# The scan states of a chunk fetched at the end of a loop turn instead of in its middle, with the scan steps spread anew over the turns

## The chip, the cores and the metric

The kernel runs on one core of a Trainium2 chip. The metric is the device time of one execution in microseconds. Five engines work side by side, each in the order of its own instruction stream: PE (matrix multiply; PEld is its weight load), DVE (vector), ACT (scalar and activation functions), POOL, and SP, which in this kernel only issues DMA transfers. They meet through semaphores. An instruction that waits holds up everything behind it on its engine.

## What is computed

The input `x` is 2 x 4096 x 256, read as 8192 tokens of 256 values. Cut to what matters:

```python
u = x @ W_in + b_in                       # 64 values a token
g = sigmoid(x @ W_gate + b_gate)
h_t = tanh(h_prev @ A + u_t @ Bm)         # scan over tokens in time
y = g * (h @ C.T + u @ D.T) + (1 - g) * x
x1 = layernorm(x + (y @ W_out + b_out + x))
hh = gelu(x1 @ (alpha1 * sign(w1)).T + b1)   # 1024 wide
out = layernorm(x1 + hh @ (alpha2 * sign(w2)).T + b2)
```

`alpha1` and `alpha2` are the mean absolute values of the rows of `w1` and `w2`. All in float32. The scan runs along each of the two sequences of 4096 tokens, from a zero state.

## The kernel before

**The scan.** Each sequence of 4096 tokens is cut into 64 segments of 64 tokens, so that the two sequences give 128 columns which are scanned side by side. One *step* (L163 to L165) is one matmul of the 128 x 128 matrix made of A and Bm with the 128 columns (PE, two passes), then a tanh on ACT that writes the next state into `st`. There are 40 warm-up steps, that bring the segments' first states near their true values, and 64 real ones: 104 in all, in the order of the list `plan`; `done` counts them. The lower half of `st` holds `u`, the upper half the states.

**The chunks.** Everything else is done in 16 chunks of 512 tokens; one chunk takes four steps' states. For a chunk c the stages are:

- `load_u` (L353) and `load_h` (L357): DMAs that copy u and the states of the chunk out of `st` into the two halves of the tile `hu` (three buffers). `load_x` (L345), `load_gate_x` (L104): x transposed. `load_n` (L362): x as rows into `xn` (four buffers; so the fetch for chunk c+3 waits until the store of chunk c-1, which leaves from the same buffer, has landed).
- `gate`: matmuls `ps_g` and a tanh `tg` (L372). `mix`: two output tiles `ps_y` from `hu` and `cd` (L381, four matmul passes), the add of a row to `xn` on POOL (L366), then d on DVE (L388); `mix_end` (L393, L396).
- `project`: 16 matmul passes `ps_z` (L406), then x1 (L417) and its statistics (L262, L266, L271, and on POOL L272). `shift` (L277) and `norm` (L285, four ACT passes).
- `blocks`: a transpose in blocks of 32 on DVE (L456) and 16 DMAs of 32 KB on the SP queue (L462) which put x1 transposed into `xlo`; `split_hi` (L470, ACT) and `split_lo` (L474, DVE) cut it in two parts.
- `up` in four pieces (8 matmul passes L493 each; gelu L503 and a cast L512 on ACT), `low` (L519, DVE), `down` in four pieces (16 matmuls L535 each), the scaling L551, `add` (L557), `stats`, and `store`: `shift`, four ACT passes (L285), the output DMA (L572, SP).

**The order.** It is written out by hand in the loop `for c in range(end)` (c = 0 to 14), and no scheduler changes it: each engine's instructions stand in the order in which the program emits them, SP's DMAs included. A turn c works at the same time on the up and down products of chunk c, the last half of down and the store of chunk c-1, norm and blocks of chunk c+1, mix and project of chunk c+2, and the fetches of chunk c+3. For turn c, left to right in the order of the text:

norm and blocks c+1; up 0; down 2 of c-1; **mix c+2**; mix_end; **load c+3** (u, then states); load_x; up 1; step; down 3 of c-1; add, stats of c-1; gate; up 2; step; split_hi c+1; store c-1; **load_n c+3**; down 0; project c+2; up 3; step; down 1.

`step()` (L680) emits one step if there is one left. `do(i, "load")` first emits steps until all states of chunk i are in the plan's past, then the two DMAs. In turns 10 and 11 one more step stands just ahead of `mix`. So the loop begins with 66 steps done; turns 0 to 9 hold three steps, turns 10 and 11 four, and from turn 12 on there are none.

Of the kernel before, what the change touches and what calls it, by code (L numbers as in the profile page):

```python
# [37 lines left out]
def gated_recurrence_then_binary_ffn(  # L38
# [61 lines left out]
    def load_xT(c, pieces=1):  # L100
        x_tiles[c] = xp.tile([P, KD, N], FP, tag="xt", name=f"xt{c}", bufs=XTB)
        for k in range(pieces):
            cut = slice(k * KD // pieces, (k + 1) * KD // pieces)
            nc.sync.dma_start(out=x_tiles[c][:, cut, :], in_=xT[c][:, cut, :])  # L104
# [53 lines left out]
    def idle_products(n):  # L158

        for _ in range(n):  # L160
            nc.tensor.matmul(p_h, ones, ones, start=True, stop=True)
# [20 lines left out]
    def count():  # L182
        nc.tensor.matmul(p_h[0:1, 0:1], ones[:, 0:1], cnt[:, 0:1], start=True, stop=True)
        nc.vector.tensor_copy(flag, p_h[0:1, 0:1])
# [59 lines left out]
    def mean_w2():  # L244
        ps = p_1.tile([P, N], FP, tag="h", name="ps_al2")
        nc.tensor.matmul(ps[:, :DM], ones, al2[:, 0, :], start=True, stop=True)
        nc.vector.tensor_scalar(al2_r, ps[:, :DM], 1.0 / H, None, ALU.mult)
        yield
# [396 lines left out]
    ch = [Chunk(c, f"{c}") for c in range(NC)]  # L645
# [8 lines left out]
    def ready():  # L654
        return done < len(plan) and plan[done] // SPC in have_u

    def next_steps():
        nonlocal done
        steps(plan[done])
        done += 1  # L660
        if done == WARM:
            first_states()
        for i in range(3):
            if done == WARM + (i + 1) * SPC:
                ch[i].load_h()
        if waiting and not held:
            for what, args in waiting:
                what(*args)
            waiting.clear()

    def emit(what, pieces, pace=5600):
        nonlocal since
        for _ in pieces:
            since += COST.get(what, 0)
            if since >= pace:
                since = min(since - pace, pace // 2)
                if ready():
                    next_steps()

    def step():  # L680
        if ready():
            next_steps()

    def do(i, what, *args, pace=5600):
        if not 0 <= i < len(ch):
            return
        if what == "load":
            need = WARM + (ch[i].c + 1) * SPC
            while done < need:
                next_steps()  # L690
            ch[i].load_u()
            ch[i].load_h()
        elif what in ("load_n", "load_x", "load_gate_x"):
            getattr(ch[i], what)()
        else:
            emit(what, getattr(ch[i], what)(*args), pace)
# [4 lines left out]
    def parts(n, pace):  # L701
        emit("part", (next(stream) for _ in range(n)), pace)
# [31 lines left out]
    with tc.manual_schedule(engines={ET.PE, ET.Activation, ET.DVE, ET.Pool, ET.SP}):  # L734
        waiting = []
        for c in range(FIRST + 1, FIRST + 6):
            load_xT(c)
        idle_products(7)
        emit("u", u_of_chunks((FIRST,)), 1 << 30)
        since = 0  # L740
        for p in range(48):
            for visit in VISITS.get(p, ()):
                emit("", u_of_chunks(*visit))
                emit("u", [None], EARLY)
            for what, *args in AROUND.get(p, ()):
                what(*args)
            parts(1, EARLY)
        assert done >= WARM + SPC, done
        for i in range(6):
            ch[i].xt = x_tiles[i]  # L750
        ch[0].in_x = ch[1].in_x = True
        parts(1, 600)
        do(0, "mix", pace=850)
        do(0, "mix_end")
        held = True
        parts(2, 600)
        assert done >= WARM + 2 * SPC, done
        do(1, "mix", pace=850)
        do(1, "mix_end")
        held = False  # L760
        do(0, "project", 0, p_2, "o", pace=1700)
        do(0, "project", 1, pace=1700)
        do(0, "stats1")
        assert done >= WARM + 3 * SPC, done
        do(2, "mix", pace=1700)
        do(0, "shift")
        do(1, "project", 0, p_2, "o", pace=1700)
        do(0, "norm")
        do(1, "project", 1, pace=1700)
        do(1, "stats1")  # L770
        parts(2, 1700)
        while waiting:
            next_steps()
        waiting = None
        do(0, "turn", True)
        emit("", mean_w2())
        mixed = ch[2].mix_end()
        next(mixed)
        do(1, "norm", nc.vector)
        do(0, "rest")  # L780
        next(mixed)
        parts(3, 1700)
        end = len(ch) - 1
        parts_met = compare()
        since = -1 << 40
        size[0] = TB
        for c in range(end):
            far = 0 < c < end - 1
            if far:
                do(c + 1, "shift")  # L790
                do(c + 1, "norm")
                do(c - 1, "low", 3)
                do(c + 1, "blocks")
            do(c, "up", 0)
            if c == end - 1:
                do(c - 1, "low", 3)
                do(c + 1, "shift")
                do(c + 1, "norm")
            do(c - 1, "down", 2)
            if c > 0:  # L800
                if c in (10, 11):
                    step()
                do(c + 2, "mix")
            do(c, "low", 0)
            mixed = ch[c + 2].mix_end() if 0 < c < end - 1 else iter(())
            next(mixed, None)
            if c == end - 1:
                assert done == len(plan), done
                next(parts_met)
                next(parts_met)  # L810
            do(c + 3, "load")
            do(c + 6, "load_x")
            if c > 0 and c % 2 == 0:
                do(10 + c // 2, "load_gate_x")
            do(c, "up", 1)
            step()
            do(c - 1, "down", 3)
            next(mixed, None)

            if c <= 12 or c == end - 1:  # L820
                do(c - 1, "add")
            if c <= 12:
                do(c - 1, "stats")
            if 2 <= c <= 12:
                emit("gate", (next(stream) for _ in range(KD)))
            if c == 0:
                do(c + 1, "turn")
            do(c, "low", 1)
            if c == end - 2:
                do(c - 1, "add")  # L830
            if c > 12:
                do(c - 1, "stats")
            if c == end - 1:
                next(parts_met)
                next(parts_met)
            if c < end - 2:
                do(c + 1, "rest")
            do(c, "up", 2)
            if c == end - 1:
                do(c + 1, "turn")  # L840
                do(c + 1, "rest")
            step()
            if far:
                do(c + 1, "split_hi")
            do(c, "low", 2)
            if c < end - 2:
                do(c - 1, "store", range(TB), nc.scalar)
            do(c + 3, "load_n")
            do(c, "down", 0)
            do(c + 2, "project", 0)  # L850
            if c == end - 2:
                do(c + 1, "split_lo")
                ch[c - 1].st2.shift(range(TB))
            do(c + 2, "project", 1)
            if far and c < end - 2:
                do(c + 1, "split_lo")
            do(c + 2, "stats1")
            if c == end - 2:
                do(c + 1, "rest")
            do(c, "up", 3)  # L860
            if c >= end - 2:
                do(c - 1, "store", range(TB), nc.scalar)
            step()
            do(c, "down", 1)
        count()
        do(end, "up", 0)
        do(end - 1, "low", 3)
        do(end, "low", 0)
        do(end - 1, "down", 2)
        do(end - 1, "down", 3)  # L870
        do(end, "up", 1)
        do(end - 1, "add")
        do(end - 1, "stats")
        do(end, "low", 1)
        do(end, "up", 2)
        do(end, "low", 2)
        do(end, "down", 0, True)
        do(end, "up", 3, True)
        do(end - 1, "store", range(TB), nc.scalar)
        do(end, "low", 3, True)  # L880
        do(end, "down", 1)
        do(end, "down_end")
# [64 lines left out]
```

## Time and profile before

| | us |
|---|---|
| median of 3 runs | 434.62 (433.52 to 434.92) |
| the profiled execution, its own time | 433.8 |
| its span (first to last instruction) | 431.9 |
| from one `mix` to the next, turns 2 to 13 (127.08 to 371.77) | 22.24 in the mean |

| engine | busy us | share of the span |
|---|---|---|
| PE | 421.8 | 98% |
| PEld | 343.0 | 79% |
| DVE | 334.9 | 78% |
| ACT | 283.1 | 66% |
| POOL | 162.6 | 38% |

How to read it: the span is that of one profiled execution; 1.9 us lie around it. The chain of work that ended last is followed back from the last instruction, at each step to what released it. In an answer in order of time a row has the start, the duration, the engine, the line, the operation and what it writes from what; SPq stands for the issue of a DMA on the SP queue, not for its transfer. In the page's DMA rows the last number is the median time from issue to landing. In the answer on waits a row has the waiting engine and line, what released it, the time in total, the number of waits and the longest.

### The profile page before, as it was taken

The page shows a single profiled execution, that of the slowest core. Times are in us where ns is not written, and L with a number is a line of the kernel's source. Part 1 is how long each engine was busy: PE and PEld are TensorE (multiplying, and loading weights), DVE is VectorE, ACT ScalarE, POOL GpSimd, SP SyncE. Part 2 cuts the span into 40 slices and gives each one's busy share as a digit, 9 for nine tenths or more (in the row PEclk, how much of TensorE's full clock was granted, in tenths as well). Part 3 has the DMA queues.
Part 4 walks back from the last instruction along what each step waited for, and adds up shares of the span by engine and source line. Part 5 has one row for each costly group of instructions (what it writes and reads, how often), then busy time and mean ns, then how long its engine had stood idle before and what let it go on. Part 6 is the DMA issues. An engine that isn't in the chain of part 4 may idle for free.

```text
span 431.9 us, 6782 instructions
## 1 busy us (share of the span) xinstructions
PE 421.8 (98%) x2390; PEld 343.0 (79%) x2390; DVE 334.9 (78%) x569; ACT 283.1 (66%) x472; POOL 162.6 (38%) x176
## 2 busy tenths in 40 slices
PE   8999999999999999999999999999999999999992
PEld 6576667788978888887878787979797888889981
DVE  0255377885979797979898888888797979799684
ACT  3353533486576777767676867677777685859881
POOL 1000013564143545353535454534343444415513
PEclk9999999999999999999999999999999999999996
DMA  8894555000251625161525242524242232311102
GB/s 288 312 286 181 159 154 176 1 2 0 45 176 41 219 52 179 42 227 36 155 65 187 78 143 77 191 74 146 71 128 87 58 115 58 114 34 50 49 2 102
DMA packets 30902, 49.24 MB, mean 114 GB/s; under 512 B 5264, under 2 KB 19600, under 8 KB 30864
## 3 DMA queue, kind: packets, MB, share of 16 engines
q1 hardware_dynamic: 30288, 48.39, 35.7%
q8 instruction: 21, 0.34, 0.3%
q10 hardware_dynamic: 576, 0.37, 0.3%
q14 instruction: 17, 0.14, 0.1%
HBM read 29.33 MB, written 8.39 MB: 87 GB/s over the span
## 4 chain that ended last, share of the span: by engine, by line
PE 96%; DMA 1%; DVE 1%; ACT 0%; SPq 0%; POOLq 0%; POOL 0%; issue 0%; DVEq 0%
PE ps_h L493 27%; PE ps_o L535 26%; PE ps_g L320 13%; PE ps_z L406 13%; PE ps_y L381 6%; PE ps_s L164 6%; PE ps_u L138 3%; DMA w_gate<-in_W_gate 1%; PE ps_t L437 1%; PE ps_p L535 0%; DVE hlo L519 0%; DVE bs_b L262 0%; SPq L104 0%; ACT h L503 0%; POOLq L886 0%; POOL rs_b L272 0%
## 5 line engine op out<-in xcount | busy, mean ns | idle before, releaser
L535 PE MATMUL ps_o<-sg,hhi 128*128 128x256 f32 x496 | 120.5, 284 | 0.0
L535 PE MATMUL ps_o<-sg,hlo 128*128 128x256 f32 x496 | 117.4, 278 | 0.1
L503 ACT ACTIVATE h<-ps_h,bias_c,al 128x512 f32<-128x512 f32 x128 | 95.0, 770 | 14.9 <-PE ps_h L493 10.7
L366 POOL TENSOR_TENSOR xn<-xn,bo_r 128x256 f32<-128x256 f32 x64 | 59.0, 955 | 100.6 <-DMA xn<-in_x 97.6
L535 PEld LDWEIGHTS ps_o<-sg,hhi 128*128 128x128 f32 x496 | 93.4, 188 | 1.4 <-DVE o L551 0.4
L535 PEld LDWEIGHTS ps_o<-sg,hlo 128*128 128x128 f32 x496 | 93.4, 188 | 1.4 <-DVE hlo L519 0.3
L493 PE MATMUL ps_h<-xhi,sg 128*128 128x512 f32 x256 | 92.7, 443 | 0.0
L519 DVE TENSOR_TENSOR hlo<-h,hhi 128x1024 fp32r<-128x1024 f32 (+1 forms) x65 | 79.9, 1247 | 4.9 <-ACT hhi L512 4.6
L493 PE MATMUL ps_h<-xlo,sg 128*128 128x512 f32 x256 | 79.8, 393 | 0.0
L512 ACT CAST hhi<-h 128x1024 fp32r<-128x1024 f32 (+1 forms) x65 | 67.4, 1039 | 2.0
L272 POOL TENSOR_TENSOR rs_b<-rs_b,neg_half 128x4 f32<-128x4 f32 (+1 forms) x17 | 28.1, 1655 | 102.0 <-DVE rs_b L271 97.0
L320 PE MATMUL ps_g<-xt,w_gate 128*128 128x384 f32 (+3 forms) x212 | 66.1, 425 | 0.3 <-DMA w_gate<-in_W_gate 0.3
L493 PEld LDWEIGHTS ps_h<-xhi,sg 128*128 128x128 f32 x256 | 46.5, 189 | 18.6 <-issue 9.8
L165 ACT ACTIVATE st<-ps_s 64x128 f32<-64x128 f32 x104 | 27.8, 267 | 45.0 <-PE ps_s L164 44.6
L493 PEld LDWEIGHTS ps_h<-xlo,sg 128*128 128x128 f32 x256 | 48.0, 188 | 11.1 <-DVE xlo L474 0.2
L366 POOL TENSOR_TENSOR xn<-xn,b_r 128x256 f32<-128x256 f32 x64 | 55.4, 895 | 1.9 <-PE ps_t L437 1.9
L406 PE MATMUL ps_z<-w_out,tg 128*128 128x256 f32 x224 | 50.7, 379 | 0.0
L164 PEld LDWEIGHTS ps_s<-st,wab 128*128 128x128 f32 x208 | 35.4, 189 | 19.1 <-ACT st L165 10.1
L406 PEld LDWEIGHTS ps_z<-w_out,tg 128*128 128x128 f32 x224 | 41.4, 190 | 5.1
L470 ACT CAST xhi<-xlo 128x1024 fp32r<-128x1024 f32 x13 | 13.7, 1051 | 42.4 <-DMA xlo<-xb 26.6
L164 PE MATMUL ps_s<-st,wab 128*128 128x128 f32 x208 | 40.6, 277 | 0.1
L320 PEld LDWEIGHTS ps_g<-xt,w_gate 128*128 128x128 f32 x212 | 33.2, 191 | 7.2 <-issue 5.3
(79 smaller groups left out, 485.2 us busy)
## 6 DMA issues: line engine op xcount, KB each, us to landing
xt<-in_xT SPq DMA_DIRECT2D x31, 512.0 KB, 4.3
xn<-in_x SPq DMA_DIRECT2D x16, 512.0 KB, 3.2
out_y<-xn SPq DMA_DIRECT2D x15, 512.0 KB, 2.6
xlo<-xb SPq DMA_DIRECT2D x208, 32.0 KB, 1.9
hu<-st SPq DMA_DIRECT2D x32, 128.0 KB, 2.3
w1t<-in_w1T SPq DMA_DIRECT2D x2, 512.0 KB, 5.8
w1n<-in_w SPq DMA_DIRECT2D x2, 512.0 KB, 6.7
w2t<-in_w2T SPq DMA_DIRECT2D x2, 512.0 KB, 6.5
```

The lines of the kernel that those rows point to most:

```text
L164: nc.tensor.matmul(p_h, ab, st[:, j].rearrange("p b k -> p (b k)"), start=True, stop=True)
L165: nc.scalar.activation(h_of[:, j + 1].rearrange("p b k -> p (b k)"), p_h[TOP, :], AF.Tanh)
L272: nc.gpsimd.tensor_tensor(rs, rs, neg_half[:, cut], ALU.pow)
L320: nc.tensor.matmul(ps[:, cut], w_gate[:, k, bass.ts(m, P)], xt_[:, k, cut], start=k == 0 and i == 0, stop=k == KD - 1, skip_group_check=True,)
L366: nc.gpsimd.tensor_tensor(r[:, i, :], r[:, i, :], row, ALU.add)
L381: nc.tensor.matmul(ps[:, m, :], cd[:, bass.ts(m, P)], self.hu, start=True, stop=True)
L406: nc.tensor.matmul(self.ps_z[:, i, :], self.y[:, k, bass.ts(i, P)], w_out[:, k, :], start=k == 0, stop=k == KD - 1,)
L493: nc.tensor.matmul(ps, sg1[:, k, bass.ts(j, P)], part[:, k, :], start=n == 0, stop=n == 2 * KD - 1,)
L503: nc.scalar.activation(to, ps.rearrange("p (a i c) -> p a i c", a=P // 32, c=32) if self.far else ps, AF.Gelu, bias=b1_c[:, j : j + 1], sc ...
L512: nc.scalar.copy(hi[:, part, :], h[:, part, :])
L519: nc.vector.tensor_sub(lo[:, i, :], h[:, i, :], hi[:, i, :].bitcast(FP))
L535: nc.tensor.matmul(ps[:, i, :], part[:, j % 2, bass.ts(tb, P)], sg2[:, j, :], start=j == 0 and part is self.h[j // 2][0] and first, stop=j ...
```

## The change

`load` is taken apart. `load_u` stays where `load` stood, in the middle of the turn. `load_h`, with the steps it makes sure of, goes to the end of the turn, between the third step and `down 1`. On the SP queue this puts L357 behind the store of chunk c-1 and behind `load_n` of chunk c+3. The extra step in turns 10 and 11 goes, and so does the second step of turn 1; the three steps stand in turn 12 instead. So a turn holds three steps, turn 1 two, until turn 12; the step's instructions are the same. L353 to L572 keep their numbers in the changed kernel.

```diff
-        if what == "load":
+        if what == "load_h":
             need = WARM + (ch[i].c + 1) * SPC
             while done < need:
                 next_steps()
-            ch[i].load_u()
             ch[i].load_h()
-        elif what in ("load_n", "load_x", "load_gate_x"):
+        elif what in ("load_u", "load_n", "load_x", "load_gate_x"):
             getattr(ch[i], what)()
...
             if c > 0:
-                if c in (10, 11):
-                    step()
                 do(c + 2, "mix")
...
-            do(c + 3, "load")
+            do(c + 3, "load_u")
             do(c + 6, "load_x")
...
-            step()
+            if c != 1:
+                step()
             if far:
                 do(c + 1, "split_hi")
...
             step()
+            do(c + 3, "load_h")
             do(c, "down", 1)
```

## The prediction

> **What bounds the kernel now.** I read the chain of work that ended last first, then the busy time by stretch of the main loop, then the SP queue and the matrix engine in order of time.
>
> ```profile
> span 431.9 us, 6782 instructions
> PE 421.8 (98%) x2390; PEld 343.0 (79%) x2390; DVE 334.9 (78%) x569; ACT 283.1 (66%) x472; POOL 162.6 (38%) x176
> PE 96%; DMA 1%; DVE 1%; ACT 0%; SPq 0%; POOLq 0%; POOL 0%; issue 0%; DVEq 0%
> xn<-in_x SPq DMA_DIRECT2D x16, 512.0 KB, 3.2
> out_y<-xn SPq DMA_DIRECT2D x15, 512.0 KB, 2.6
> xlo<-xb SPq DMA_DIRECT2D x208, 32.0 KB, 1.9
> hu<-st SPq DMA_DIRECT2D x32, 128.0 KB, 2.3
> ```
>
> 96% of the chain is PE, so PE's own order sets the time. The table of stretches says the same of the loop: in the turns from 125 to 414 us PE is busy in all of every stretch (22.40 of 22.40, 22.30 of 22.30, 21.70 of 21.70), at a granted clock of 1.00. Nothing is hidden there: PE has no idle time to give back, and each microsecond that it is made to wait in the loop goes straight to the end. From the DMA rows keep the landing times, counted from issue: 3.2 us for `xn`, 2.3 for a half of `hu`.
>
> The last turn that matters, c = 12, on the SP queue and then on PE:
>
> ```profile
> 362.58 0.60 SPq L353 DMA_DIRECT2D hu<-st  x1
> 363.28 0.54 SPq L357 DMA_DIRECT2D hu<-st  x1
> 367.12 0.35 SPq L572 DMA_DIRECT2D out_y<-xn  x1
> 369.78 0.33 SPq L362 DMA_DIRECT2D xn<-in_x  x1
> 373.58 10.48 SPq L462 DMA_DIRECT2D xlo<-xb  x16
> ```
> ```profile
> 371.77 1.88 PE L381 MATMUL ps_y<-hu,cd 128*128 128x512 f32 x4
> ```
> ```profile
> SPq L572 <- ACT xn L285: 36.3, 13, 6.8
> SPq L362 <- DMA out_y<-xn: 29.3, 12, 3.4
> ```
>
> The reader is to see: the states (L357) are issued 8.5 us ahead of the matmul that reads them (L381, `mix` of chunk 15, in turn 13). The `xn` fetch (L362) is issued only 2.0 us ahead of it, because it reuses the buffer that the store (L572) writes out, and waits 2.66 us for that store to land. The store in turn waits for ACT.
>
> **Part 1, the steps.** PE's order has 38 steps in the loop before and after, 104 in all. One leaves turn 1, one each leaves turns 10 and 11, and three enter turn 12. On PE a step shows as a hole of 0.22 us between its neighbours (turn 11: the step starts at 327.57, `mix` at 327.79), wherever it stands. Sum: -3 x 0.22 + 3 x 0.22 = 0. In none of the 38 places does PE wait for the step before (that wait, 10.1 us in 30 cases on the page of waits, is 0.2 us in one case after 84 us), since steps stand 3.8 us or more apart. ACT's 0.27 us tanh moves likewise. In turn 12 ACT is busy 15.67 of 21.70 us, so three more are covered; uncovered they would cost 0.8 us.
>
> **Part 2, `load_u`.** It stays in place. With L357 gone from behind it, the next fetches (L345, L104) go 0.64 us sooner, and are needed turns later: nothing. The store is not drawn forward: SP stands idle ahead of L572 in every turn, waiting for ACT.
>
> **Part 3, `load_h`, the whole price.** SP issues in order. In the changed order the states of chunk c+3 come directly behind `load_n` of c+3 (L362), which itself stands behind the store's landing. So their issue cannot come before that of L362, n, plus 0.35 to 0.40 us. The last tanh that turn 12's fetch needs falls at about 369.8 by ACT's queue (the cast that ends 369.51, then 0.27), not later than n: no further delay. Behind `load_h` on SP stand the 16 `xlo` fetches, which wait for DVE's transpose until 3.4 us or more after n: not delayed. Behind the waiting `mix` stands all of PE.
>
> When do the states land? Lower end: 0.40 + 2.3 = n + 2.7, as if alone. Upper end: behind the 512 KB of `xn`, n + 3.3 + 0.6 = n + 3.9. The nearest row is two 512 KB fetches issued back to back at 142.54 and 143.17 (L345, L104): they land 4.0 and 4.5 us after issue, that is at 146.54 and 147.67, 1.13 us apart, against 3.5 us for a single one issued at 163.99. The second is served after the first. So I take 3.2 for `xn` and about 0.5 us for 128 KB more (32 KB land in 1.9, 128 KB in 2.3: 0.4 us for 96 KB): **n + 3.7**.
>
> The page "DMA: Bandwidth & Descriptors" of the Trainium skill, section "Queues, rings and completion order", speaks against the change too: descriptors on each DMA engine are consumed in ring order. By it the sum would use n + 3.7, without it n + 2.7; the pair of rows above decides without the page.
>
> Lateness against the trace, turn by turn (start of `mix` minus n gives the gap; late = 3.7 - gap):
>
> turn of `mix`: n, start, gap, late
> 2: 126.18, 127.08, 0.90, 2.80
> 3: 149.03, 149.33, 0.30, 3.40
> 4: 169.79, 171.57, 1.78, 1.92
> 5: 191.63, 193.82, 2.19, 1.51
> 6: 214.18, 216.07, 1.89, 1.81
> 7: 236.96, 238.31, 1.35, 2.35
> 8: 258.96, 260.56, 1.60, 2.10
> 9: 280.46, 282.81, 2.35, 1.35
> 10: 302.69, 305.27, 2.58, 1.12
> 11: 325.04, 327.79, 2.75, 0.95
> 12: 348.14, 350.08, 1.94, 1.76
> 13: 369.78, 371.77, 1.99, 1.71
>
> If each were paid in full: 22.8 us. But a stall in turn c moves turn c+1's `mix` too, while n of turn c hangs mainly on `project` of the turn before, by `norm`, the transpose (L456) and 11 us of `xlo` issue to `split_hi` (L470) and the store's ACT pass (L285). So the last stall is deducted from the next lateness. Not without limit: that ACT pass also needs `nm_b` (L277), which hangs on this turn's PE work. Its end stands 0.4 to 1.5 us ahead of the pass, 0.9 in the mean, and DVE's backlog ahead of it adds about 0.3; I let the deduction reach 1.2 us. Then the stalls are 2.80, 2.20, 0.72, 0.79, 1.02, 1.33, 0.90, 0.45, 0.67, 0.28, 1.48, 0.51: **13.2 us**. The profiled execution took 433.8 us (span 431.9 and 1.9 around it); 433.8 + 13.2 = **447.0**. It lies 0.8 under the median of 434.62, which I leave as spread.
>
> Does PE's clock fall in stalls this long? In the tail, 420 to 424 us holds 0.77 us without a matmul at clock 1.00, and 424 to 432 us none at all at 0.59. I cost it at nothing; the longest stall expected, 2.8 us, lies between these. The Trainium skill's page "TensorE: Matmul & The Clock Gate", section "What's actually happening", puts the fall at an idle window of about 3.4 us; by that only a stall longer than any of mine would cost more.
>
> **Rivals.**
> - *Main, 0.62.* Landing at n + 3.7 with deduction: 447.0. With an unlimited deduction (only the two-turn path counts) the same lateness gives 11.5 us, 445.3. For it: the pair of fetches; against: no 128 KB copy behind a 512 KB fetch is in the trace.
> - *The states are not held up behind `xn`, 0.17.* Landing at n + 2.7: stalls 1.80, 1.20, 0.51, 0.30, 1.05, 0.05, 0.30, 0.76, together 6.0 us: 439.8. For it: the 2.3 us row; against: the pair.
> - *Nothing is deducted, 0.16.* If the store's pass waits for this turn's PE work each time, every lateness is paid: 433.8 + 22.8 = 456.6. For it: ACT waits for `nm_b` ahead of L470 in two turns; against: it waits for `xlo` in seven.
> - *Not slower, 0.05: the fetch lands in time.* Place: the same wait of `mix`. With a landing of n + 1.5 or less almost only turns 2 and 3 would wait, about 1.2 us together. At the best even the three steps taken off turns 1, 10 and 11 count and those of turn 12 are free: -0.7 us, 433.1. Against it: the shortest landing on the page is 1.9 us for 32 KB, and even that plus 0.4 is late in turns 2 and 3 by 1.4 and 2.0.
> - That the change doesn't do what it says is excluded by the order: steps stand three to a turn, two in turn 1, to turn 12, and L357 stands behind L362 in every turn from 0.
>
> **How the numbers follow.** Predicted is the main case. The range takes in both bounds of the landing and of the deduction: 439.8 to 456.6, rounded to 439.5 and 457; only "not slower" is outside. 0.3% of 434 us is 1.3 us, about what a measurement of this kernel can tell from no change. Only the fourth case lies within or under that: slower 0.95, same 0.03, faster 0.02.
>
> **What would show it.** Right: PE idle ahead of L381, released by the DMA `hu<-st`, in most of twelve turns and largest in turns 2 and 3; L357 0.4 us behind L362 on SP; that DMA's landing up from 2.3 to about 3.3 us; PE's busy time unchanged; the chain showing some 3% of DMA `hu<-st`. Wrong: a landing still at 2.3 us (second case), or stalls near the full lateness each turn (third), or a granted clock under 1.00 inside the loop, which I cost at nothing.

## The result, and the profile after

The changed kernel takes 452.93 us (median of 6 runs, 450.85 to 453.51), the one before 434.50 us (6 runs): 1.0417 times as long, with a 95% interval from 1.0398 to 1.0436. The profiled execution took 453.51 us, 19.7 more than that of before, and its span is 451.7 us, 19.8 more.

The page of the changed kernel: the span, the busy times, the chain that ended last by engine, and three DMA rows (the last number is the time from issue to landing).

```profile
span 451.7 us, 6779 instructions
PE 426.8 (94%) x2390; PEld 345.1 (76%) x2390; DVE 325.8 (72%) x569; ACT 284.7 (63%) x472; POOL 146.1 (32%) x176
PE 47%; DMA 14%; DVE 13%; SPq 12%; ACT 8%; issue 4%; POOL 1%; POOLq 0%; DVEq 0%; ACTq 0%
...
xn<-in_x SPq DMA_DIRECT2D x16, 512.0 KB, 3.6
out_y<-xn SPq DMA_DIRECT2D x15, 512.0 KB, 2.6
...
hu<-st SPq DMA_DIRECT2D x32, 128.0 KB, 2.6
```

PE does the same 2390 instructions but is no longer the chain: 47% of it instead of 96%, and the rest is shared among the DMAs, the SP queue, DVE and ACT. PE's idle time is the span less its busy time: 24.9 us instead of 10.1. So 14.8 of the 19.8 us are idle, and 5.0 are longer busy time, of which more below. The median of the `hu` row has risen little, since half of those 32 transfers are `load_u`, which did not move.

The waits of PE on this tile (us in total, times, longest):

```profile
PE ps_y L381 <- DMA hu<-st: 11.7, 11, 2.0
...
PE ps_y L381 <- issue: 3.1, 1, 3.1
```

That is the whole 14.8 us, in twelve waits, one for each `mix` of turns 2 to 13. The 3.1 us of turn 2 are the same wait, for which the profile names no releaser: its states are issued at 127.03 and land 3.7 us later, and `mix` starts at 130.83.

Turn 12 on the SP queue, and `mix` of turn 13 on PE, as they were shown of before:

```profile
385.12 0.34 SPq L572 DMA_DIRECT2D out_y<-xn  x1
387.80 0.34 SPq L362 DMA_DIRECT2D xn<-in_x  x1
388.23 0.55 SPq L357 DMA_DIRECT2D hu<-st  x1
```
```profile
392.03 1.99 PE L381 MATMUL ps_y<-hu,cd 128*128 128x512 f32 x4 [0.74 <-DMA hu<-st]
```

The states (L357) are now issued 3.8 us ahead of `mix` instead of 8.5, directly behind the rows (L362). The chain of waits in the stretch from 196 to 204 us has the mechanism from end to end (start, duration, what):

```profile
195.80 0.99 ACT xn L285 x2
...
196.81 2.62 DMA out_y<-xn
...
199.49 0.33 SPq L362
...
199.87 3.79 DMA hu<-st
...
203.71 0.70 PE ps_y L381
```

Read downwards: ACT's last pass of the store, the store's landing, the issue of the rows fetch into the buffer that the store has left, then 3.79 us for the states, then PE.

Measured from the rows issue, n, to the start of `mix`, the twelve turns give 4.18, 4.36, 3.90, 4.22, 4.15, 4.14, 3.89, 4.34, 4.31, 4.21, 4.21 and 4.23 us: 4.2 in the median, where the prediction had 3.7.

### The profile page after: what moved, and what is told of

It is laid out like the page before. It is cut to its first block, busy times and chain, and to the rows that moved or that the text cites. A ratio compares the mean times of both kernels' runs of the same rounds, so it can differ in the third digit from the quotient of the medians.

```text
span 451.7 us, 6779 instructions
## 1 busy us (share of the span) xinstructions
PE 426.8 (94%) x2390; PEld 345.1 (76%) x2390; DVE 325.8 (72%) x569; ACT 284.7 (63%) x472; POOL 146.1 (32%) x176
## 4 chain that ended last, share of the span: by engine, by line
PE 47%; DMA 14%; DVE 13%; SPq 12%; ACT 8%; issue 4%; POOL 1%; POOLq 0%; DVEq 0%; ACTq 0%
SPq L462 11%; PE ps_h L493 10%; PE ps_g L320 9%; PE ps_o L535 9%; ACT xn L285 6%; DMA hu<-st 6%; PE ps_z L406 5%; DMA out_y<-xn 5%; PE ps_y L381 5%; PE ps_s L164 4%; PE ps_u L138 3%; DVE hlo L519 2%; DMA xlo<-xb 2%; DVE bs_b L262 1%; DVE xb L456 1%
## 5 line engine op out<-in xcount | busy, mean ns | idle before, releaser
L535 PE MATMUL ps_o<-sg,hhi 128*128 128x256 f32 x496 | 120.8, 285 | 0.0
L535 PE MATMUL ps_o<-sg,hlo 128*128 128x256 f32 x496 | 117.6, 278 | 0.1
L535 PEld LDWEIGHTS ps_o<-sg,hlo 128*128 128x128 f32 x496 | 93.5, 189 | 1.3 <-DVE hlo L519 0.3
L535 PEld LDWEIGHTS ps_o<-sg,hhi 128*128 128x128 f32 x496 | 93.5, 188 | 0.9
L519 DVE TENSOR_TENSOR hlo<-h,hhi 128x1024 fp32r<-128x1024 f32 (+1 forms) x65 | 77.2, 1205 | 4.9 <-ACT hhi L512 4.8
L366 POOL TENSOR_TENSOR xn<-xn,bo_r 128x256 f32<-128x256 f32 x64 | 45.7, 745 | 96.9 <-DMA xn<-in_x 81.1
L493 PEld LDWEIGHTS ps_h<-xhi,sg 128*128 128x128 f32 x256 | 47.1, 191 | 19.2 <-issue 11.3
L366 POOL TENSOR_TENSOR xn<-xn,b_r 128x256 f32<-128x256 f32 x64 | 52.2, 846 | 1.9 <-PE ps_t L437 1.9
L164 PEld LDWEIGHTS ps_s<-st,wab 128*128 128x128 f32 x208 | 35.6, 189 | 19.2 <-ACT st L165 10.2
L381 PE MATMUL ps_y<-hu,cd 128*128 128x512 f32 x64 | 32.3, 623 | 14.8 <-DMA hu<-st 11.7
L285 ACT ACTIVATE xn<-xn,nm_a,rs_a 128x256 f32<-128x256 f32 x60 | 31.2, 591 | 19.3 <-DVE nm_a L277 19.3
```

Of the source, the lines that this page charges most:

```text
L164: nc.tensor.matmul(p_h, ab, st[:, j].rearrange("p b k -> p (b k)"), start=True, stop=True)
L285: nc.scalar.activation(r, r, AF.Identity, bias=self.sh[:, i : i + 1], scale=rs)
L366: nc.gpsimd.tensor_tensor(r[:, i, :], r[:, i, :], row, ALU.add)
L381: nc.tensor.matmul(ps[:, m, :], cd[:, bass.ts(m, P)], self.hu, start=True, stop=True)
L493: nc.tensor.matmul(ps, sg1[:, k, bass.ts(j, P)], part[:, k, :], start=n == 0, stop=n == 2 * KD - 1,)
L519: nc.vector.tensor_sub(lo[:, i, :], h[:, i, :], hi[:, i, :].bitcast(FP))
```

## The experiments

**The theories.** A: the fetch of the states is late because it stands on SP behind the rows fetch, which waits for the store to land and then occupies the DMA engines with 512 KB; the new places of the steps cost nothing. Rivals: the steps carry part of the loss (B); the place at the end of the turn is late in itself (C); the queueing behind 512 KB is no cause (D). Two finer theories: a fall of the clock after a wait adds to the loss (E), and a lateness is reduced by the stall of the turn before (F, against G: every late fetch costs its own share).

**1. The fetch moved alone.**

```diff
+                if c in (10, 11):
+                    step()
                 do(c + 2, "mix")
...
-            if c != 1:
-                step()
+            step()
```

(against the changed kernel). 

> The fetch of the states moved to the end of the turn, with the steps as they were before the change (three a turn, four in turns 10 and 11). Theory A (the fetch arrives late behind the rows fetch, the steps cost nothing): 452.9 us as the whole change, within 1.5 us; the wait of mix on the DMA hu is still there, some 15 us in all. Rival B (the new places of the steps carry a part of the loss): nearer to 434.5 than the whole change by more than 2 us.

Measured: 453.73 us, 1.0436 times before (1.0404 to 1.0468); the waits of `mix` add up to 14.7 us. The move of the fetch is the whole loss. What is left for the steps is within the spread.

**2. The fetch ahead of the store, the steps as changed.**

```diff
+            do(c + 3, "load_h")
             if c < end - 2:
                 do(c - 1, "store", range(TB), nc.scalar)
...
             step()
-            do(c + 3, "load_h")
             do(c, "down", 1)
```

> The steps as after the change, the fetch of the states as before the store of the turn instead of behind the rows fetch (the last one makes turn 12's third step come right behind its second). Theory A: the fetch is issued some 6 us earlier and lands in time, so 434.5 us, up to 1 us more for the two steps in a row in turn 12. Rival B (the steps): above 436 us.

Measured: 436.57 us, 1.0038 (1.0022 to 1.0054): 1.9 us above before, more than either the 1 us allowed by A or nothing. By the bound set down, this speaks for B. The trace places it elsewhere. No `mix` waits, and from turn to turn the time between two starts of `mix` is that of before within 0.3 us in turns 2 to 12. The loss is in turn 12 alone, where this edit puts two steps in a row and PE waits for the first one's tanh (start, duration and, in brackets, the wait ahead of it):

```profile
361.47 0.66 PE L164 MATMUL ps_s<-st,wab 128*128 128x128 f32 x2 [1.90 <-ACT st L165]
```

ACT had that tanh standing behind a gelu and a cast, which ran from 358.48 to 361.24. The profiled execution, at 438.6 us the slowest of the ten, shows a second thing: the granted clock of PE is 0.50 from 361.65 to 365.06, just behind this wait, which makes the turn's PE work 1.7 us longer (experiments 6 and 8 come back to this). So the loss belongs to this kernel's pair of steps; the changed kernel has no such wait (0.1 us ahead of all its steps). My allowance for the pair was too small. The states land slowly in this kernel too, 3.8 to 5.3 us after their issue in turns 2 to 11, where one or two 512 KB fetches of x stand just ahead of them on SP. It costs nothing, because their issue is 6.4 to 8.3 us ahead of `mix`.

**3. The two fetches exchanged**: `load_n` behind `load_h`, both at the end of the turn.

```diff
-            do(c + 3, "load_n")
             do(c, "down", 0)
...
             do(c + 3, "load_h")
+            do(c + 3, "load_n")
             do(c, "down", 1)
```

> As the changed kernel, but the fetch of the rows (load_n) is put behind the fetch of the states, both at the end of the turn: the states stand directly behind the store. Theory A (what makes it late is standing behind the rows fetch, which waits 2.66 us for the store to land and brings 512 KB): the states land about 3.2 us after the store's issue, that is 0.5 us after the time when the rows fetch was issued; late only in turn 3 by 0.2 us: 434.7 us. Rival C (the place behind the store, at the end of the turn, is late in itself): 440 us or more.

Measured: 434.30 us, 0.9992 (0.9978 to 1.0007), no difference from before. Turn 3, the one in which the expectation had the states late, on the SP queue and on PE in order of time:

```profile
145.82 0.34 SPq L572 DMA_DIRECT2D out_y<-xn  x1
146.26 0.72 SPq L357 DMA_DIRECT2D hu<-st  x1
148.73 0.33 SPq L362 DMA_DIRECT2D xn<-in_x  x1
```
```profile
149.78 1.88 PE L381 MATMUL ps_y<-hu,cd 128*128 128x512 f32 x4
```

Here the states go out 2.5 us ahead of the rows and land after 2.8 us, at 149.1; `mix` finds them there, 0.7 us later. It is closer in two other turns: in turn 2 they land 0.2 us ahead of `mix`, and in turn 13 `mix` starts 0.04 us after they land, its weight load having waited 0.15 us for them. With the steps and the end of the turn as in the changed kernel and only two neighbours on one queue exchanged, the loss is gone: A stands, and B and C fall.

**4. The rows fetch cut in two**, 128 KB ahead of the states and 384 KB behind them.

```diff
-            do(c + 3, "load_n")
+            do(c + 3, "load_n_first")    # xn[:, 0:1, :]
...
             do(c + 3, "load_h")
+            do(c + 3, "load_n_rest")     # xn[:, 1:, :]
             do(c, "down", 1)
```

> As the changed kernel, but the rows fetch is cut in two: 128 KB ahead of the states, as before waiting for the store to land, and 384 KB behind them. It parts the two terms of the lateness: the issue behind the store's landing stays, the queueing behind 512 KB goes. Theory A with both terms: the states land about 2.9 us after the first rows issue instead of 4.2, the stalls add up to 7.3 us: 441.8 us. Rival D (the queueing is no cause, the states land slowly for another reason): 452.9 us as the whole change.

Measured: 443.30 us (441.83 to 444.93), 1.0204 (1.0158 to 1.0251). Of the four runs two took 441.8 or 441.9 us, as expected, and two 444.7 or 444.9, at a lower mean clock (0.990 and 0.991 against 0.993 and 0.995); the profile is of the fastest. Issue to landing of one turn's two transfers, first in this kernel, then in the changed one:

```profile
xn<-in_x SPq DMA_DIRECT2D x1, 128.0 KB, 2.5
hu<-st SPq DMA_DIRECT2D x1, 128.0 KB, 2.6
```
```profile
xn<-in_x SPq DMA_DIRECT2D x1, 512.0 KB, 3.8
hu<-st SPq DMA_DIRECT2D x1, 128.0 KB, 3.8
```

Behind 128 KB the states land in 2.6 us, behind 512 KB in 3.8, and before the change, in the middle of the turn, in 2.3. So D falls: of the 18.4 us about half (452.93 - 443.30 = 9.6) come from the transfer ahead, and the rest (443.30 - 434.5 = 8.8) from being issued behind the store's landing. These are shares in this order of taking away; as one turn's wait shortens the next, they need not be the same in another. This kernel also shows the reduction F bare. From turn 3 to turn 11 `mix` (L389 here) waits in every second turn only:

```profile
152.06 1.98 PE L389 MATMUL ps_y<-hu,cd 128*128 128x512 f32 x4 [1.01 <-DMA hu<-st]
174.45 1.88 PE L389 MATMUL ps_y<-hu,cd 128*128 128x512 f32 x4
197.79 1.96 PE L389 MATMUL ps_y<-hu,cd 128*128 128x512 f32 x4 [0.94 <-DMA hu<-st]
220.12 1.88 PE L389 MATMUL ps_y<-hu,cd 128*128 128x512 f32 x4
```

A turn that has waited gives the next turn's fetch that much more time.

**5. Late fetches in the even turns alone**, on the steps of experiment 1.

```diff
             do(c + 3, "load_u")
+            if c % 2:
+                do(c + 3, "load_h")
...
             step()
-            do(c + 3, "load_h")
+            if c % 2 == 0:
+                do(c + 3, "load_h")
```

> The states fetched late in the even turns alone, and in the middle of the turn in the odd ones, with the steps as before the change: six of the twelve late fetches. Theory F (a lateness is reduced by the stall of the turn before, up to 1.2 us): the waits of turns 3, 5, 7, 9, 11 and 13 are paid in full, with the measured landing of 4.2 us 3.9 + 2.0 + 2.9 + 1.9 + 1.5 + 2.2 = 14.3 us: 448.8 us. Rival G (each late fetch costs its share, nothing is reduced): half of 18.4 us, 443.7 us.

Measured: 450.27 us, 1.0360 (1.0341 to 1.0379). Two waits of this kernel:

```profile
152.54 3.63 PE L381 MATMUL ps_y<-hu,cd 128*128 128x512 f32 x4 [3.36 <-DMA hu<-st]
176.62 1.88 PE L381 MATMUL ps_y<-hu,cd 128*128 128x512 f32 x4
```

Half of the late fetches cost 15.8 of 18.4 us: F, not G. The waits alone say the same: six here add up to 13.2 us, twelve in the changed kernel to 14.8. The rest is in part the clock, which fell twice in this execution, after the waits of 3.36 and 2.38 us. In turn 3, PE waits 3.36 us instead of 2.03, as nothing is deducted.

**6. PE kept at work while it waits, in turns 2 and 3.** Against the changed kernel:

```diff
             if c > 0:
+                if c in (2, 3):
+                    idle_products(8)
                 do(c + 2, "mix")
```

First what this is about, in the changed kernel: two stretches that hold the wait of turn 2 (127.75 to 130.83), one that holds the wait of turn 3 (153.31 to 155.34), and the one behind it. The columns are the stretch, its length, then busy time of PE, PEld, DVE, ACT, POOL, then the granted clock and the DMA share and GB/s.

```profile
125.61:129.02 3.41, 2.13 (x18) 1.89 (x16) 1.33 (x3) 2.94 (x7) 1.02 (x1) 1.00 0.53 192
129.02:132.44 3.42, 1.61 (x5) 0.87 (x5) 1.25 (x1) 2.46 (x4) 2.12 (x4) 1.00 0.20 70
152.92:156.33 3.41, 1.38 (x7) 0.74 (x6) 1.25 (x1) 2.88 (x5) 1.55 (x3) 1.00 0.39 127
156.33:159.74 3.41, 3.41 (x8) 1.99 (x7) 1.58 (x2) 0.00 (x0) 1.23 (x2) 0.50 0.22 48
```

The clock is at 0.50 for 3.41 us and at 1.00 on both sides of them; over somewhat wider stretches the mean reads as about 0.7, which is the figure in the expectation below. The turn's PE work takes 24.20 us instead of 22.5 in its neighbours: 1.7 us more, half of 3.41.

> As the changed kernel, with eight idle products (about 1.8 us of matmuls whose result nobody reads) ahead of mix in turns 2 and 3, so that PE works while it waits for the states. They fit into the waits of 3.1 and 2.0 us. Theory E (in turn 3 the granted clock falls to 0.7 for some 4 us and costs 1.7 us, because PE had stood still): the clock stays at 1.00, 451.2 us or less in all runs, as the runs of the changed kernel at 450.9. Rival: the fall has nothing to do with the waiting: 452.9 us, with the clock's fall in the profile.

Measured: 452.17 us (451.61 to 455.73). In turns 2 and 3 the clock stayed at 1.00, but in the profiled execution it fell in turn 8 instead, after a wait of 1.94 us, in which no products stood; the states of that turn took 5.0 us to land (stretch of turn 8; PE busy 24.25):

```profile
273.50:298.80 25.30, 24.25 (x126) 19.40 (x127) 18.03 (x32) 15.43 (x25) 7.55 (x9) 0.93 0.37 114
```

So there was no fall where PE was kept at work, which one execution does not show to be the rule, and the time did not come to 451.2 in all runs. The expectation failed.

**7. Idle products in all late turns**: eight in turns 2 and 3, four in turns 4 to 14.

```diff
+                if c > 1:
+                    idle_products(8 if c < 4 else 4)
                 do(c + 2, "mix")
```

> As the changed kernel, with idle products ahead of mix in all late turns: eight in turns 2 and 3 (1.9 us), four in turns 4 to 14 (1.0 us), so that PE stands still for at most 1.2 us at a time. Theory E (each fall of the clock follows a standstill of some 1.7 us or more and costs 1.7 us): no fall in the loop in any run, mean clock 0.995 or more, all runs within 1.5 us of one another near 451.5 us (450.9 as the runs without a fall, and up to 0.6 us where four products are longer than the wait). Rival (the falls come without regard to the waits): the spread of the changed kernel stays, 450.9 to 455, with clocks down to 0.988.

Measured: 453.25 us (452.96 to 454.37). All loop turns of the profiled execution are at clock 1.00, and the runs lie within 1.5 us of one another, as expected; the time is not as expected, nor is the mean clock, 0.993 to 0.996 where 0.995 or more was expected (the kernel before has 0.992 to 0.996 in its runs). 1.0 us of it is a fault of the edit: turn 14 has no `mix`, and its four products fill no wait. The other 452.2 are still above the 450.9 of the two runs of the changed kernel with the highest mean clock. What a fall costs at the end is left open here: 1.7 us of PE work is seen in its turn, but a longer turn also leaves the next fetch more time.

**8. The changed kernel again.** 

> The changed kernel once more beside these on the same chip: 452.9 us. For the landing times and the clock in a second profile: the stalls of mix add up to 14.8 us again; if the clock falls in turn 3 the time is near 453.3, if it does not near 450.9.

Measured: 453.44 us (452.89 to 455.03). The waits of `mix` add up to 15.2 us, and the clock fell in two turns, 2 and 10:

```profile
130.30:156.20 25.90, 24.18 (x127) 19.33 (x127) 18.38 (x32) 15.60 (x26) 8.44 (x11) 0.93 0.36 113
321.50:346.50 25.00, 24.20 (x126) 19.27 (x126) 17.79 (x32) 15.18 (x25) 8.45 (x11) 0.93 0.32 95
```

The falls do not stand in fixed turns. They fit as one cause of the spread of over 2 us among runs of the same kernel: of its first six runs the two at 450.9 and 451.0 us have a mean clock of 0.996, the four at 452.7 to 453.5 one of 0.988 to 0.992.

What the falls go by can be read from the traces. The clock changes only at points that lie a whole number of slots of 3.413 us apart: here it is full for 187.73 us between the two falls, 55 slots, and each fall inside the loop lasts one slot at 0.50. Laid out in these slots, all ten executions agree, from the first full clock to the last: it falls behind every slot in which PE stood still for 1.90 us or more, and behind none in which it stood still for 1.86 us or less. In the rows of experiment 6 the wait of 3.08 us is split by the end of a slot, 1.28 us on one side and 1.80 on the other, and nothing falls; the wait of 2.03 us lies whole in one slot, and the clock falls. This is read from the runs afterwards; none was made to test it.

## Why the prediction was right, and where it was short

It had 447.0 us in a range of 439.5 to 457.0, slower with 0.95; measured are 452.9. The mechanism, the turns and the direction were right, and the loss was short by 6 us.

- *What bounds it.* Right: PE had no slack, and every wait of `mix` went to the end.
- *The steps.* Right at zero, by experiments 1 and 3.
- *The issue behind L362.* Right: L357 starts 0.38 to 0.43 us behind it in every turn, predicted 0.35 to 0.40.
- *The landing, n + 3.7.* The direction was right (behind `xn`, not beside it), the size was short, and above the upper end of 3.9. I added 0.5 us for 128 KB to the 3.2 us in which `xn` had landed by itself. In the changed kernel `xn` takes 3.5 to 3.8 us with the states behind it, and the states land 0.3 to 0.6 us after it, 3.5 to 3.8 from their own issue. So the 0.5 held; the 3.2 was too short for a transfer with another behind it. `mix` starts at n + 4.2. By the prediction's own rule the stalls are then 3.30, 2.70, 1.22, 0.81, 1.50, 1.65, 1.40, 0.65, 0.97, 0.48, 1.78 and 1.01, together 17.5 us instead of 13.2. This is the mis-sized term: 4.3 of the 6 us.
- *The deduction.* Right in kind (experiments 4 and 5), and about right in size. The time from the start of `mix` to the rows issue of the same turn was shorter than before by 1.80 of 3.08 us of waiting in turn 2, by 1.31 of 1.27 in turn 5, by 1.56 of 1.59 in turn 7, but by nothing of 1.35 in turn 9, nor of 2.03 in turn 3, where the clock fell. With a landing of n + 2.95, as experiment 4 had it, the rule gives 7.6 us; there `mix` of turn 13 started 8.1 us later than before.
- *The clock, costed at nothing.* Wrong, and a clock under 1.00 in the loop was the prediction's own sign of that. It fell to 0.50 for 3.41 us after a wait of 2.03 us, and PE lost 1.7 us in that turn. The wait expected there was 2.2, and I had put that between two rows of the tail which were too wide to tell. The page "TensorE: Matmul & The Clock Gate" of the Trainium skill, section "What's actually happening", puts the fall at an idle window of about 3.4 us; here it came after waits of 2.03, 1.94 and 1.91 us and stayed away after one of 3.08, so a wait shorter than that window does not exclude it. Read finer, the tail of before has a fall after a short standstill: the last matmul ends at 423.31, and the clock falls at 425.40, 2.09 us later.

```profile
421.99:425.40 3.41, 1.32 (x12) 1.12 (x10) 3.24 (x12) 0.62 (x2) 2.17 (x3) 1.00 0.40 159
425.40:428.81 3.41, 0.00 (x0) 0.00 (x0) 1.13 (x6) 0.47 (x1) 0.70 (x1) 0.50 0.48 154
```

- *Two smaller readings*, on which nothing came to hang: the `xlo` fetches follow n by 2.8 us in turn 3 (149.03, 151.84), not by 3.4 or more in every turn, and two steps of turn 0 stand 2.9 us apart (89.85, 92.78), not 3.8.
- 17.5 and 1.7 are 19.2 us; the twelve turns took 19.8 more than before (285.46 against 265.68 us from `mix` of turn 1 to that of turn 13). The page of the changed kernel splits the span's 19.8 into 14.8 of idle time and 5.0 of busy time; PE's busy time was forecast unchanged; 1.7 of the 5.0 are the fall, and the rest is 0.2 to 0.3 us in each turn. That would fit the end of the matmul ahead of the wait, which the next one no longer covers (a matmul of L535 lasts 0.28 us, and the next one starts 0.11 or 0.12 us behind it); no run tests it.

Of the rivals, "nothing is deducted" at 456.6 came nearer to the measured time than the main case (3.7 us off against 5.9), by luck: its lateness was too small and its reason is excluded by experiment 5.

## What to carry to other kernels

On a queue that issues in order, a small fetch that somebody waits for must not stand behind one that waits for a buffer to come free: it inherits that wait, and then the bytes of the other as well; here the exchange of the two neighbours was worth 18.6 us (452.9 against 434.3). Before moving a fetch, write down when its new predecessor is issued and when its reader starts, turn by turn; in a loop whose late transfer hangs on work two turns back, a lateness is not paid in every turn, so that curing half of the late turns may cure almost nothing. For the landing behind another transfer, take it longer than the sum of the single rows: here it was n + 4.2 to the reader's start, where 3.2 and 0.5 had been added.

## What the runs showed of the hardware

- Landing of the same 128 KB from its own issue, by what was issued about 0.4 us ahead of it: 2.3 us with 128 KB ahead (before, L353 and L357, 0.7 us apart), 2.5 to 2.9 behind 128 KB from `in_x`, 2.8 or 2.9 behind the 512 KB store (once 3.9), 3.5 to 3.8 behind the 512 KB fetch (3.7 to 4.1 in experiments 1 and 8). In experiment 2, with the fetches ahead issued 0.5 to 0.7 us apart, it is 2.2 or 2.3 behind no 512 KB fetch, 3.8 to 4.2 behind one, 4.6 to 5.3 behind two. The transfer ahead is slowed too: 3.1 to 3.4 us before, 3.5 to 3.8 with the states behind it.
- The granted clock fell to 0.50 for 3.41 us at a time inside the loop, eight times in six executions, at single waits of 1.9 to 3.4 us, and not at others as long: at 2.03 and not at 3.08 in one execution, at 1.94 and not at 2.01 in another. What parts them is PE's idle time within one slot of 3.41 us on a fixed grid: 1.90 us or more in each slot ahead of a fall, 1.86 or less in all others at full clock, in ten executions (experiment 8 has the working).
